# Sums of squares of a layer norm: from VectorE reductions to TensorE products in column groups, in the output stage of a fused triangle and spectral kernel

## The chip, the cores and the metric

One core of a Trainium2 chip runs the whole kernel. The metric is the device time of one execution in microseconds. A core has five engines with a queue each: TensorE (PE, with its weight loads as PEld), VectorE (DVE), ScalarE (ACT), GpSimd (POOL) and SyncE (SP, which here issues DMAs). An engine runs its queue in order, and waits at an instruction until what it needs has been signalled.

## The reference

The input x is 512 x 512 tokens of 64 channels, in f32. Two layers follow one another, each added to its input after a group norm (`_gn`) over the whole image:

```python
# layer 0, on xn = layer norm of the group-normed x
left  = (xn @ left_w  + left_b)  * mask * sigmoid(xn @ lgate_w + lgate_b)
right = (xn @ right_w + right_b) * mask * sigmoid(xn @ rgate_w + rgate_b)
out_gate = sigmoid(xn @ ogate_w + ogate_b)
out = einsum('bkjd,bkid->bijd', left, right)
out = _ln(out, onorm_w, onorm_b) @ out_w + out_b
x = x + out * out_gate
# layer 1: 12 x 12 lowest Fourier modes of the group-normed x, mixed over channels, and back
x = x + real(ifft2(mix(fft2(_gn(x))[:12, :12])))
```

The mask is 1 where both tokens of a pair are valid; the sum over k runs over valid rows alone, and a masked output pair is the layer norm of zero, so that its `out` is one constant row.

## The kernel before, in words

Rows with a valid mask, at most 256 of 512, are ranked to the front, so that the triangle product is computed in a 256 x 256 square ("compact"). The kernel runs in stages: statistics of x and copying of the valid tokens; the projections left and right; the triangle product; the stage of u; the output stage; the spectral mixing; and the last stage, which adds the inverse transform and writes the output. The change lies in the stage of u (686 to 794 us in the profile) and, above all, in the output stage (794 to 1485 us).

**Steps and units.** The code that does both stages is one loop over steps, `for s in range(-LEAD, total_g + 2 * SIZE)`. A step handles 8 tokens of each of 128 rows, 512 columns of a tile; eight steps (`SIZE`) make a unit of 64 tokens by 128 rows. The first 8 units (`first`) belong to the stage of u: they apply the output norm and out_w to the triangle product and write the result to u in memory (`u_d`). The 32 others are the output stage. A unit is a pair (jc, half): 32 columns jc of the image, and two of the four blocks of 128 ranked rows. Blocks 0 and 1 hold the valid rows, blocks 2 and 3 the masked ones. Before, half 0 was blocks 0 and 1 and half 1 was blocks 2 and 3, and half 1 came first, save for the last jc. A unit is also split into four chunks c of 16 tokens: c 0 and 1 are its first block, c 2 and 3 its second.

**What a step does**, with the line of the profile:

- TensorE transposes four 128x128 squares of the input of step s+13 into PSUM (`t_ps`, L969), and ScalarE copies them out, minus the mean of the group norm, as `xt_c` (L974).
- TensorE multiplies `xt_c` of step s by the gate's weights: `w_ps`, four matmuls in which `xt_c` is the stationary operand and `gate_x` moves (L979, in `times`).
- TensorE centers the channels of step s+12 in the same manner with the matrix `center_x`: `c_ps` (L979, in `centered`). The tokens are then on the partitions and the channels along the free axis. ScalarE squares it (L1004), and in every second step VectorE sums the squares over the channels of two steps (L1012, into `scratch`).
- Once a unit, at step 5, ScalarE takes the root of the sums (L1018), and VectorE the reciprocal at step 7 (L1188): the factor `rs_n` of the layer norm. ScalarE must load another table for the root and again for the sigmoid that follows.
- VectorE multiplies `w_ps` by the factor (L1195) and in odd steps adds the gate's bias (L1201) to get `z_t` of a chunk. ScalarE takes its sigmoid in even steps (L1146).
- GpSimd multiplies `z_t` by u, or by the row `bias_row_out` in masked blocks (L1038, `gated`), and adds the result to the input that lies in `places` (L1042, `added`). It also issues the gathers of the next input (L629).
- TensorE takes the Fourier transform over the rows of the unit before: `f_ps`, at steps 0 and 4, as four matmuls of 512 columns in the four groups of 32 columns of the array (L1069, `tile_position`); ScalarE copies it out every second unit (L1077).
- VectorE gathers statistics for the second group norm (L1097), four instructions a step, and joins them once in four units.
- SP loads the slots of u for jc+1 (L1029, 32 DMAs of 64 KB) at step 4 of every second unit, and stores finished tiles (L1058).

**What sets the order.** The block runs under `tc.manual_schedule()`: each engine gets its instructions in the order in which the loop writes them. Within a step ScalarE's order is xt_c, the sigmoid (even steps), the root (step 5), the square, the copy of f_ps. TensorE's is t_ps, w_ps, c_ps, f_ps.

**Buffers.** PSUM[...]: t_ps 2, scratch 1, f_ps 1, c_ps 2, w_ps 2. `z_t` has four buffers in SBUF, sq_c two of 16 x 64.

## Time and profile before

| What | us |
|---|---|
| median of 3 runs (1837.78 to 1840.75) | 1838.84 |
| profiled execution, whole time | 1839.54 |
| its span on the core | 1837.7 |
| stage of u in it | 686 to 794 |
| output stage in it | 794 to 1485 |
| TensorE busy in the span | 1637.7 (89%) |
| VectorE busy | 1423.6 (77%) |
| ScalarE busy | 961.9 (52%) |
| GpSimd busy | 945.3 (51%) |

The span runs from the first to the last instruction of the program, and 1.8 us of the profiled time lie around it. Busy shares are of the whole span; what binds one stage must be read inside it. A row of the profile's groups gives line, engine, operation, what is written and read, shapes and count, then the busy time and the mean of one instruction in ns. A row of a timeline has the start in us, the length in us, and the group; `x8` are eight instructions run together. An f32 matmul leaves two records[...], so four matmuls read as x8; a transpose leaves one.

### The profile page before, as it was taken

The numbers are of one execution on the slowest core, as the hardware profiler recorded it, in microseconds if no ns is written. First come the engines' busy times: TensorE is split into PE (matmuls) and PEld (weight loads), VectorE is DVE, ScalarE is ACT, GpSimd is POOL, SyncE is SP. The second block draws the span as 40 slices with busy tenths as digits, with TensorE's granted clock in tenths as the row PEclk, the third lists the DMA queues.
The fourth block names the chain that finished last, engine by engine and source line by source line (L and its number), as shares of the span: only waits on it lengthen the run. The fifth ranks groups of instructions, "written<-read, shape, count | busy, mean of one in ns | idle before, by whom it ended". The sixth has DMA issues, their size and how long they took to land.

```text
span 1837.7 us, 33577 instructions
## 1 busy us (share of the span) xinstructions
PE 1637.7 (89%) x11414; PEld 1287.7 (70%) x11414; DVE 1423.6 (77%) x2973; ACT 961.9 (52%) x1708; POOL 945.3 (51%) x711
## 2 busy tenths in 40 slices
PE   6779799999799999999999999999999866998772
PEld 5667666665678878897788888888888744665441
DVE  5989777777455547788999999999999975675552
ACT  3555555555222259976777777777777631111000
POOL 3666211111000006788999999999999862211110
PEclk9989899999899999999999999999999966555555
DMA  6999255556656513667777876776777698999999
GB/s 255 381 375 371 106 127 138 138 138 154 208 174 182 177 41 141 224 234 257 254 244 249 279 269 233 241 274 234 253 258 258 210 273 338 411 426 426 427 427 379
DMA packets 188453, 467.94 MB, mean 255 GB/s; under 512 B 34672, under 2 KB 134000, under 8 KB 147184
## 3 DMA queue, kind: packets, MB, share of 16 engines
q1 hardware_dynamic: 157376, 262.21, 42.5%
q0 software_dynamic: 27712, 201.40, 29.1%
q10 hardware_dynamic: 3184, 2.08, 0.4%
q8 instruction: 93, 1.52, 0.3%
q14 instruction: 88, 0.72, 0.1%
HBM read 278.05 MB, written 187.56 MB: 253 GB/s over the span
## 4 chain that ended last, share of the span: by engine, by line
PE 29%; DVE 16%; DMA 9%; POOL 4%; issue 3%; ACT 1%; DVEq 0%; POOLq 0%; ACTq 0%
PE c_ps L979 6%; PE w_ps L979 6%; PE t_ps L969 5%; PE l_ps L1348 4%; DVE stats2c L1097 4%; DMA places<-x_h,dst_i 4%; PE y_ps L990 4%; DVE z_t L1195 3%; DVE scratch L1012 3%; DVE z_t L1201 3%; PE f_ps L1069 2%; POOL z_t L1038 2%; DMA out_x<-places 2%; POOL places L1042 2%; DMA lx_t<-x_h,dst_i 2%
## 5 line engine op out<-in xcount | busy, mean ns | idle before, releaser
L979 PE MATMUL w_ps<-gate_x,xt_c 128*128 128x128 f32 x2048 | 280.1, 280 | 32.1 <-DVE z_t L1195 26.7
L1042 POOL TENSOR_TENSOR places<-places,z_t 128x1024 f32<-128x1024 f32 x127 | 301.2, 2371 | 8.0
L979 PEld LDWEIGHTS w_ps<-gate_x,xt_c 128*128 128x128 f32 x2048 | 251.5, 194 | 47.8 <-DVE z_t L1195 43.4
L979 PE MATMUL c_ps<-center_x,xt_c 128*128 128x128 f32 x2048 | 276.2, 278 | 1.2 <-ACT xt_c L1008 0.6
L979 PEld LDWEIGHTS c_ps<-center_x,xt_c 128*128 128x128 f32 x2048 | 252.1, 194 | 3.9 <-ACT xt_c L974 2.3
L1348 PE MATMUL l_ps<-places,rinv 24*128 24x512 f32 x512 | 207.8, 1124 | 29.3 <-DVE places L1355 18.6
L1097 DVE BATCH_NORM_STATS2 stats2c<-places 128x6 f32<-128x128 f32 x1024 | 220.5, 278 | 12.5 <-POOL places L1042 12.5
L1012 DVE TENSOR_REDUCE scratch<-sq_c 128x16 f32<-128x1024 f32 x160 | 194.6, 1216 | 27.9 <-ACT sq_c L1007 18.7
L1146 ACT ACTIVATE z_t<-z_t 128x1024 f32<-128x1024 f32 x128 | 135.5, 1059 | 133.7 <-DVE z_t L1201 116.0
L1199 POOL TENSOR_TENSOR z_t<-z_t,bias_row_out 128x1024 f32<-128x1024 f32 x32 | 75.7, 2365 | 246.6 <-DVE z_t L1195 242.5
L969 PE MATMUL t_ps<-c_ident,places 128*128 128x128 f32 x1280 | 199.0, 278 | 1.3 <-DVE places L854 1.3
L1348 PEld LDWEIGHTS l_ps<-places,rinv 24*128 24x128 f32 x512 | 120.3, 303 | 111.9 <-DVE places L1355 59.6
L969 PEld LDWEIGHTS t_ps<-c_ident,places 128*128 128x128 f32 x1280 | 144.5, 142 | 60.6 <-issue 50.3
L974 ACT ACTIVATE xt_c<-t_ps,ab_xc 128x512 f32<-128x512 f32 x256 | 176.0, 687 | 10.7 <-PE t_ps L969 9.8
L1195 DVE TENSOR_TENSOR z_t<-w_ps,rs_n 128x512 f32<-128x512 f32 x256 | 171.9, 672 | 3.7 <-PE w_ps L979 3.5
L1004 ACT ACTIVATE sq_c<-c_ps 128x512 f32<-128x512 f32 x256 | 150.5, 588 | 30.9 <-PE c_ps L979 29.4
L679 DVE BATCH_NORM_STATS2 stats1c<-x_ps 128x6 f32<-128x512 f32 x256 | 155.6, 681 | 12.5 <-PE x_ps L678 12.2
L1201 DVE TENSOR_TENSOR z_t<-z_t,scratch 128x1024 f32<-128x1024 f32 x128 | 156.3, 1221 | 10.0 <-ACT rs_n L1018 3.8
L1038 POOL TENSOR_TENSOR z_t<-z_t,places 128x1024 f32<-128x1024 f32 x64 | 151.6, 2369 | 16.2 <-ACT z_t L1146 13.3
L1355 DVE TENSOR_TENSOR places<-places,l_ps 128x512 f32<-128x512 f32 x176 | 110.2, 683 | 56.1 <-DMA places<-x_h,dst_i 45.5
L1038 POOL TENSOR_TENSOR z_t<-z_t,bias_row_out 128x1024 f32<-128x1024 f32 x63 | 149.4, 2371 | 4.6 <-ACT z_t L1146 4.0
L733 POOL COPY rbc<-rq_out 128x512 f32<-128x512 f32 x64 | 38.3, 613 | 210.0 <-DVE rq_out L209 132.0
(212 smaller groups left out, 2748.8 us busy)
## 6 DMA issues: line engine op xcount, KB each, us to landing
x_h<-places SPq DMA_DIRECT2D x64, 1024.0 KB
out_x<-places SPq DMA_DIRECT2D x44, 1024.0 KB
places<-u_d SPq DMA_DIRECT2D x512, 64.0 KB
out_x<-lx_t SPq DMA_DIRECT2D x20, 1024.0 KB
left_d<-o_c SPq DMA_DIRECT2D x64, 256.0 KB
right_d<-o_c SPq DMA_DIRECT2D x64, 256.0 KB
left_raw<-left_d SPq DMA_DIRECT2D x64, 256.0 KB
right_raw<-right_d SPq DMA_DIRECT2D x64, 256.0 KB
```

Of the source, the lines that this page charges most:

```text
L679: nc.vector.bn_stats(stats[:, 0, 16 * (jc % quarter) + 4 * r + c, :], ps.rearrange("p i k -> p (i k)"))
L969: nc.tensor.transpose(tps[:, i, :], flat[:, o : o + P], ident)
L974: nc.scalar.activation(xts[s], tps, AF.Identity, bias=ab1[:, 2:3])
L979: nc.tensor.matmul(ps[:, 2 * i : 2 * i + 2, :], xts[s][:, i, :], w, start=True, stop=True)
L1004: nc.scalar.activation(sq, cps, AF.Square)
L1012: nc.vector.tensor_reduce(totals[k % 2][:, 8 * (n - 1) : 8 * (n + 1)], sqs.pop(s // 2), AX.X, ALU.add)
L1038: nc.gpsimd.tensor_mul(zs[k, c], zs[k, c], u)
L1042: nc.gpsimd.tensor_add(xr, xr, zs.pop((k, c)))
L1097: nc.vector.bn_stats(st[k // 4][:, g, k % 4, :], x_of(k)[:, :, 2 * g : 2 * g + 2])
L1195: nc.vector.tensor_mul(z[:, 8 * odd : 8 * odd + 8, :], wps, rs)
L1201: nc.vector.tensor_add(z, z, bias_ps["ogate"].unsqueeze(1).to_broadcast([P, 16, C]))
L1348: nc.tensor.matmul(ps.rearrange("p j o -> p (j o)"), rinv[h, b, :], it[h], start=True, stop=True, tile_position=(32 * g, 0),)
```

## The change

Centering in the output stage is turned around: `center_x` is the stationary operand and `xt_c` moves, so that one matmul of 512 columns makes `c_ps` with the channels on the partitions. ScalarE squares it as before. In the next step TensorE sums the squares over channels with four matmuls, one for each of the four squares of 128 tokens, in the four groups of 32 columns: the stationary operand `sum_w[:, n, :]` (128 x 32) puts the sums of step n in rows 2n and 2n+1 of its group, and the eight steps of a unit are accumulated in one bank, `row_sums`. At step 4 ScalarE copies that bank to SBUF, at step 5 TensorE turns it with one transpose into a buffer of `t_ps`, and ScalarE takes the root from there. The bank comes from c_ps, which has one buffer now. ScalarE's square stands ahead of the root in step 5.

A unit now holds one block of valid rows and one of masked rows (`block`), in the order half 0, half 1, save for the last jc, which is as before. VectorE makes the product of chunk 3 (masked, `shared`), 30 times in all, and GpSimd the other three. In the stage of u the reductions stay on VectorE but run on one step each.

```diff
-            units = [(jc, half) for jc in range(NJ) for half in ((1, 0) if jc < NJ - 1 else (0, 1))]
+            units = [(jc, half) for jc in range(NJ) for half in (0, 1)]
...
+                sum_w = lp.tile([P, SIZE, 32], F32, name="sum_w")
+                nc.scalar.dma_start(sum_w, t["c_sum_w"])
+
+                def block(k, r):
+                    jc, half = units[k]
+                    return half + 2 * r if jc < NJ - 1 else 2 * half + r
...
                     def centered(s):
                         if s >= first * SIZE:
-                            return times(ps_c, "c_ps", s, center_x)
+                            ps = ps_c.tile([P, 4, P], F32, name="c_ps")
+                            nc.tensor.matmul(ps, center_x, xts[s], start=True, stop=True)
+                            return ps
...
                     def summed(s):
                         k, n = divmod(s, SIZE)
-                        nc.vector.tensor_reduce(
-                            totals[k % 2][:, 8 * (n - 1) : 8 * (n + 1)], sqs.pop(s // 2), AX.X, ALU.add
-                        )
+                        nc.vector.tensor_reduce(totals[k % 2][:, 8 * n : 8 * n + 8], sqs.pop(s), AX.X, ALU.add)
+
+                    def summed_rows(s):
+
+                        k, n = divmod(s, SIZE)
+                        if n == 0:
+                            row_sums[k] = ps_r.tile([P, P], F32, name="row_sums")
+                        sq = sqs.pop(s).rearrange("p n c -> p (n c)")
+                        for i in range(4):
+                            nc.tensor.matmul(
+                                row_sums[k][32 * i : 32 * i + 32, :], sum_w[:, n, :], sq[:, i * P : (i + 1) * P],
+                                start=(n == 0), stop=(n == SIZE - 1), tile_position=(0, 32 * i),
+                            )
+
+                    def keep_rows(k):
+                        kept[k] = small.tile([P, P], F32, name="kept_rows", bufs=1)
+                        nc.scalar.copy(kept[k], row_sums.pop(k))
+
+                    def turn_rows(k):
+                        tps = ps_t.tile([P, 4, P], F32, name="t_ps")[:, 0, :]
+                        nc.tensor.transpose(tps, kept.pop(k), ident)
+                        by_token[k] = tps.rearrange("p (i n) -> p i n", i=4)[:, :, : 2 * SIZE]
...
+                    def shared(k, c):
+
+                        return c == 3 and block(k, 1) >= 2 and k < last
...
-                            ps_c = products.enter_context(tc.tile_pool(name="np_c", bufs=2, space=PSUM))
+                            ps_c = products.enter_context(tc.tile_pool(name="np_c", bufs=1, space=PSUM))
+                            ps_r = products.enter_context(tc.tile_pool(name="np_r", bufs=1, space=PSUM))
                             ps_w = products.enter_context(tc.tile_pool(name="np_w", bufs=2, space=PSUM))
                         if 0 <= s < total_g:
                             wps = raw(s) if k < first else times(ps_w, "w_ps", s, gate_x)
                             del xts[s]
+                        if n == 5 and first <= k + 1 < first + len(units):
+                            turn_rows(k + 1)
                         if 0 <= s + LEAD - 1 < total_g:
                             cps = centered(s + LEAD - 1)
+                        if first * SIZE <= s + LEAD - 2 < total_g:
+                            summed_rows(s + LEAD - 2)
                         if n in (0, 4) and held(1):
                             transform(v - 1, n // 4)
...
+                        if cps is not None:
+                            squared(s + LEAD - 1, cps)
+                        if n == 4 and first <= k + 1 < first + len(units):
+                            keep_rows(k + 1)
                         if n == 5 and 0 <= k + 1 < first + len(units):
                             root(k + 1)
-                        if cps is not None:
-                            squared(s + LEAD - 1, cps)
...
-                            if held(i) and (v - i, c) != (last, 3):
+                            if held(i) and (v - i, c) == (last, 3):
+                                finished()
+                            elif held(i) and not shared(v - i, c):
                                 gated(v - i, c)
                             elif held(i):
-                                finished()
+                                nc.vector.tensor_mul(
+                                    zs[v - i, c], zs[v - i, c], bias_ps["out"].unsqueeze(1).to_broadcast([P, 16, C])
+                                )
...
-                        if 0 <= s + LEAD - 2 < total_g and (s + LEAD - 2) % 2 == 1:
+                        if 0 <= s + LEAD - 2 < first * SIZE:
                             summed(s + LEAD - 2)
```

Loads, stores, the gate and the transform take their row block from `block(k, r)` instead of `2 * half + r`. `sq_c` has three buffers of 8 x 64.

## The prediction

> **What bounds the kernel now.** I read the slices of the page first, to find the stage that the change touches, then the busy time of the engines in that stage, its waits, and two timelines in it. The slices (40 of 46 us each) put the output stage in slices 17 to 32:
>
> ```profile
> PE   6779799999799999999999999999999866998772
> DVE  5989777777455547788999999999999975675552
> POOL 3666211111000006788999999999999862211110
> PEclk9989899999899999999999999999999966555555
> ```
>
> PE, DVE and POOL all show nines there and the clock is full, so taking work from one engine pays only as far as the next allows. The busy times of the steady part (26 units of 8 steps) say how near the three are; the columns are length, then PE, PEld, DVE, ACT and POOL busy:
>
> ```profile
> 883.00:1452.50 569.50, 550.66 (x4649) 486.97 (x4649) 558.61 (x1314) 422.56 (x626) 541.15 (x261) 0.99 0.74 254
> ```
>
> A unit lasts 569.5/26 = 21.9 us, in which DVE is busy 21.5, POOL 20.8, ACT 16.3. PE's 550.7 holds pipelined tails, so I take PE from starts instead (below): 20.1. The waits of the same stretch agree that DVE is the one all others wait for:
>
> ```profile
> ACT z_t L1146 <- DVE z_t L1201: 92.4, 65, 2.6
> PE w_ps L979 <- DVE z_t L1195: 13.5, 16, 2.0
> ```
>
> So **VectorE bounds it, by little**: PE has some 1.8 us of slack in a unit. The change takes from DVE and gives to PE, so the PE prices decide. PE's timeline (start, length, group), one step with f_ps and one without:
>
> ```profile
> 1178.92 1.06 PE L979 MATMUL c_ps<-center_x,xt_c 128*128 128x128 f32 x8
> 1179.90 1.07 PE L1069 MATMUL f_ps<-places,hb 128*32 128x512 f32 x8
> 1180.90 0.66 PE L969 MATMUL t_ps<-c_ident,places 128*128 128x128 f32 x4
> 1181.39 1.06 PE L979 MATMUL w_ps<-gate_x,xt_c 128*128 128x128 f32 x8
> 1182.29 1.06 PE L979 MATMUL c_ps<-center_x,xt_c 128*128 128x128 f32 x8
> 1183.18 0.60 PE L969 MATMUL t_ps<-c_ident,places 128*128 128x128 f32 x4
> ```
>
> From start to start: t_ps 0.437 us (median over the stage), w_ps 0.893, c_ps 0.893. A plain step is 2.22. f_ps is the only product here in four column groups: c_ps lasts 0.987 ahead of it (0.094 more), f_ps itself 0.996, and the t_ps after it 0.494 (0.057 more). Its two passes start 0.453 apart. A pass of 256 columns (tri_c_ps) takes 0.2155, so 512 columns stream in about 0.427; two passes are 0.853, and entering and leaving the column groups adds 0.094 + 0.026 + 0.116 + 0.057 = 0.29 us. A unit has two f_ps: 8 x 2.22 + 2 x 1.15 = 20.1 us.
>
> **What the Trainium skill says.** "TensorEngine Tiling (Array Packing)", Key Properties: changing the tiling mode drains TensorE, while different tiles run in parallel. The trace agrees: four groups of 512 columns take one group's streaming time, plus the 0.29 us just found. "ScalarE: Activation LUTs", What ACT_TABLE_LOAD costs: 1283 ns and a drain of about 1380 for each switch of set. The trace has the 1283, but the next ACTIVATE starts 12 ns later, so I use 1.28 alone.
>
> **The change, part by part**, for one unit.
>
> c_ps with fixed weights: 8 x (4 matmuls of 128 columns) become 8 x 1 of 512. By tri_c_ps a pass of 512 is 2 x 0.2155 = 0.431, so c_ps is 0.862 instead of 0.893; the weight loads it drops were hidden beside matmuls already. Gain 8 x 0.031 = 0.25 us.
>
> Row sums on PE: in every step four matmuls of 128 columns in four column groups, between c_ps and t_ps, both of the full array. Streaming 2 x 0.107 plus the 0.29 of entering and leaving is 0.51 us; x 8 = 4.1 us. Bounds: 0.39 if the 0.094 and 0.026 of entering belong to f_ps's own waits; 1.15 if groups this short do not overlap (4 x 0.213 + 0.29). Nothing points below 0.21, the streaming itself. I take 0.51. In steps 0 and 4, f_ps now follows the sums in the same mode and pays 0.88 instead of 1.15 in all: with its two, 1.76.
>
> The turn of the sums is one transpose, 0.11. Its wait on ScalarE's copy is covered: the copy is issued a step earlier, some 2 us before.
>
> PE's unit is then 8 x (0.437 + 0.893 + 0.862 + 0.507) + 1.76 + 0.11 = **23.5 us**, against 21.9 of the whole stage now.
>
> DVE: four reductions go (104 in the stretch, 126.0 us busy, 4.85 a unit), one product of 1.22 comes: 21.5 - 4.85 + 1.22 = 17.9. POOL loses one product of 2.37: 18.4. ACT gains the copy of 128x128, about 0.3 by the 128x64 root of 0.31: 16.6. None binds, so what these three win is worth nothing once PE takes 23.5.
>
> **The added wait.** c_ps goes from two buffers to one, so each c_ps waits for the square of the step before. ScalarE around the root, now:
>
> ```profile
> 1204.56 1.28 ACT L1018 ACT_TABLE_LOAD   x1
> 1205.85 0.31 ACT L1018 ACTIVATE rs_n<-scratch,eps 128x64 f32<-128x64 f32 x1
> 1206.07 0.59 ACT L1004 ACTIVATE sq_c<-c_ps 128x512 f32<-128x512 f32 x1
> 1206.54 0.59 ACT L1077 COPY places<-f_ps 128x512 f32<-128x512 f32 x1
> 1207.01 0.71 ACT L974 ACTIVATE xt_c<-t_ps,ab_xc 128x512 f32<-128x512 f32 x1
> 1207.74 1.28 ACT L1146 ACT_TABLE_LOAD   x1
> 1209.03 1.06 ACT L1146 ACTIVATE z_t<-z_t 128x1024 f32<-128x1024 f32 x1
> 1209.99 0.58 ACT L1004 ACTIVATE sq_c<-c_ps 128x512 f32<-128x512 f32 x1
> ```
>
> After the change the square of step 5 comes first, then load, root, (f_ps copy in every second unit), xt_c, load, sigmoid, square of step 6. Let c_ps of step 5 end streaming at 0. Its square starts at 0.2 (0.16 of the array's tail and 0.04 of signal) and frees ACT at 0.7; load 1.98, root 2.2, xt_c 2.78, load 4.08, sigmoid 5.05, square done at 5.65; with the f_ps copy 6.1. PE: sums, t_ps and w_ps of step 6 end at 1.84, c_ps at 2.70, and it is at c_ps of step 7 after another 1.84, at 4.54. It stalls 1.1 us, or 1.6 with the copy: **1.4 us a unit**. Behind c_ps in PE's order stand the sums, t_ps and the next w_ps, so DVE waits too and nothing is made up. Bounds: 0 if xt_c, sigmoid and square need not follow so closely, 2 if signals cost more. The other steps are clear: their even ones have the square done 1.0 us before it is needed.
>
> Unit after: 23.5 + 1.4 = **24.8 us**.
>
> **The order of blocks.** Every unit now has one gated block that reads u and one that takes the bias row. u of the first jc is needed in unit 0 step 3, not unit 1. SP's issues (64 in 43 us, some of the second set) and POOL's wait for the first set:
>
> ```profile
> 804.83 43.43 SPq L1029 DMA_DIRECT2D places<-u_d  x64
> 830.96 2.36 POOL L1038 TENSOR_TENSOR z_t<-z_t,places 128x1024 f32<-128x1024 f32 x1 [2.71 <-DMA places<-u_d]
> ```
>
> They start at 804.8, after the last u is written, whatever the order of units. POOL now has unit 0 done at 822.4. In the new order its first product waits for 16 of 32 slots (the sixteenth is issued at 813, landing about 821), its second for all, until 831. z has four buffers, so unit 1 is held: its step 2 gets a buffer at 831 + 2 x 2.37 = 835.7. PE, two steps ahead through w_ps's two buffers, is at step 4 there and at unit 2 after 4 x 3.1 us, at 848.5, instead of 833. **16 us, once**; bounds 5 (POOL's slack makes some up) and 22. Later sets are issued at step 4 of an even unit and needed at step 3 of the next even one, 15 steps or 45 us on; 32 issues take 19 us and land in 7, so they stay hidden. Gathers and stores keep their number and size.
>
> **Costed at nothing.** In the u stage (686 to 794 us) 32 reductions become 64 shorter ones: DVE is busy 86.8 of 108 us there, PE 106.5, so PE covers it; without that cover the fixed part of a reduction, under 0.1 us x 32, is 3 us. sum_w is one load on ACT's queue, hundreds of us ahead of its use. POOL's lighter load shortens the end by 2 us at most, as the last two units keep all their POOL work.
>
> **Sum.** PE is fully loaded from unit 2 to step 3 of unit 30, 28.4 units: 28.4 x 24.8 = 704 us, against 1459 - 833.5 = 625.5 now: +79. With +16 and -2: +93. On the profiled execution's 1839.5 (span 1837.7 and 1.8 around it, 0.7 above the median of the runs) that is **1933 us**.
>
> **Rivals.** (A) Entering and leaving column groups is hidden, as the weights of the sums are constant, and no stall shows. Then PE's unit is 8 x 2.405 + 1.87 = 21.1 and with 0.2 of waits 21.3: 28.4 x (21.3 - 22.0) = -20, and with half the head, +8: about 1828, faster. For it: DVE and POOL really do fall to 18. Against it: all f_ps of the stage pay the 0.29. It decides where sums and stall together stay below 2.1 us a unit: the break-even unit is 22.0 - 14/28.4 = 21.5, and 19.4 of it is all the rest. That is 0.26 a step, less than the switches alone. (B) The sums cost 0.51 but ScalarE's chain does not hold c_ps: 28.4 x 23.5 = 667, +42 + 14: about 1895. For it: the order puts the root behind the square. (C) Groups of 128 columns run one after another: 0.64 x 8 x 28.4 = 145 more, about 2078. Against it: f_ps starts its four groups within 20 ns. That the reductions stay on DVE is not possible: the program no longer has them in this stage.
>
> **Numbers.** Chances: my sum 0.50, B 0.29, C 0.06, A 0.12, no change 0.03 (A with the full 16 of the head). So faster 0.12, same 0.03, slower 0.85, with 0.2%, about 3.7 us, as what a measurement of this kernel can tell from no change. The range takes in B with its lower bounds (sums 0.41, half the stall) and my sum with signals costing more: 1850 to 1980; it leaves out A and C.
>
> **What would show it.** Right: PE without idle but at c_ps, waiting for ACT sq_c, once a unit; t_ps starting 0.5 us after the first row_sums; DVE and POOL waiting for PE; units of 24 to 25 us; POOL's wait for u near 815 to 831. Wrong: units near 21 us with DVE or POOL still full, row_sums of 0.25 us, or c_ps never waiting for ACT.

## The result, and the profile after

| | before | after |
|---|---|---|
| median, runs on the same chip | 1838.31 us (1833.35 to 1840.75) | 1957.87 us (1956.31 to 1960.05) |
| ratio, 95% interval | | 1.0662 [1.0641, 1.0683] |
| span of the profiled execution | 1837.7 | 1954.4 |
| unit 2 starts (VectorE's reciprocal of its factor) | 833.5 | 852.9 |
| from there to unit 31 | 638.9 | 736.2 |
| the rest | 365.3 | 365.3 |

The change costs 6.6%. The last three rows split the 116.7 us between the two spans: 19.4 are lost ahead of unit 2, 97.3 over the next 29 units (25.4 us a unit instead of 22.0), and nothing after them. A run can be split like this wherever one instruction marks each turn of a loop; here it is the reciprocal, one for each unit.

The slices of the page after, a slice being 48.9 us. In slices 17 to 33 the nines of DVE and POOL have become sevens, while PE keeps its own:

```profile
PE   6779899998999999899999999999999975898873
DVE  6889677775555478367777777767777784676542
POOL 3665111110000057577777677777777773111110
PEclk9989899998999999999999999999999996555555
```

The busy times of 26 steady units (columns as in the prediction: length, PE, PEld, DVE, ACT, POOL) give 18.8 us a unit for DVE, 18.5 for POOL and 17.2 for ACT, of a unit of 25.5. VectorE and GpSimd were relieved and now idle for more than a quarter of each unit, so the loss sits in the engine that took the work or in one that it waits for:

```profile
877.90:1541.00 663.10, 627.43 (x5093) 390.02 (x5092) 488.17 (x1231) 448.21 (x650) 480.89 (x234) 0.99 0.63 214
```

The waits of the stage from 900 to 1550 us say who (total, times, longest). VectorE now waits for TensorE, where it was the other way round, and TensorE's matmuls wait above all for the square of the single `c_ps`, 23 times:

```profile
DVE z_t L1243 <- PE w_ps L986: 147.0, 115, 3.5
...
PE c_ps L992 <- ACT sq_c L1010: 35.7, 23, 1.8
```

TensorE's timeline shows both prices. L1029 are the sums of a step:

```profile
1204.02 1.02 PE L992 MATMUL c_ps<-xt_c,center_x 128*128 128x512 f32 x2
1204.97 0.43 PE L1029 MATMUL row_sums<-sq_c,sum_w 128*32 128x128 f32 x8
1205.33 0.66 PE L976 MATMUL t_ps<-c_ident,places 128*128 128x128 f32 x4
1205.82 1.06 PE L986 MATMUL w_ps<-gate_x,xt_c 128*128 128x128 f32 x8
1206.71 1.02 PE L992 MATMUL c_ps<-xt_c,center_x 128*128 128x512 f32 x2
...
1208.52 1.06 PE L986 MATMUL w_ps<-gate_x,xt_c 128*128 128x128 f32 x8
1210.85 1.12 PE L992 MATMUL c_ps<-xt_c,center_x 128*128 128x512 f32 x2 [1.27 <-ACT sq_c L1010]
```

From start to start a plain step is 2.70 us (1204.02 to 1206.71), and the eight records of the sums, 0.214 us of streaming, take 0.505 of it: 0.094 more on `c_ps`, 0.356 of their own, 0.056 more on `t_ps`. In step 7 of the unit `w_ps` to `c_ps` is 2.33 instead of 0.893. ScalarE's timeline says why: the square of step 6 (1210.21) stands behind the root, two table loads and the sigmoid, and `c_ps` starts 0.06 us after it ends:

```profile
1205.14 0.60 ACT L1010 ACTIVATE sq_c<-c_ps 128x512 f32<-128x512 f32 x1 [1.23 <-PE c_ps L992]
1205.75 1.28 ACT L1048 ACT_TABLE_LOAD   x1
1207.05 0.32 ACT L1048 ACTIVATE rs_n<-t_ps,eps 128x64 f32<-128x64 f32 x1
1207.26 0.68 ACT L981 ACTIVATE xt_c<-t_ps,ab_xc 128x512 f32<-128x512 f32 x1
1207.96 1.28 ACT L1188 ACT_TABLE_LOAD   x1
1209.25 1.06 ACT L1188 ACTIVATE z_t<-z_t 128x1024 f32<-128x1024 f32 x1
1210.21 0.58 ACT L1010 ACTIVATE sq_c<-c_ps 128x512 f32<-128x512 f32 x1
```

### The profile page after: what moved, and what is told of

The parts are those of the page before. It is cut to its first block, busy times and chain, and to the rows that moved or that the text cites. A ratio compares the mean times of both kernels' runs of the same rounds, so it can differ in the third digit from the quotient of the medians.

```text
span 1954.4 us, 34397 instructions
## 1 busy us (share of the span) xinstructions
PE 1730.5 (89%) x11958; PEld 1164.1 (60%) x11958; DVE 1343.2 (69%) x2907; ACT 994.2 (51%) x1740; POOL 877.2 (45%) x681
## 3 DMA queue, kind: packets, MB, share of 16 engines
q8 instruction: 97, 1.59, 0.3%
## 4 chain that ended last, share of the span: by engine, by line
PE 48%; DMA 13%; POOL 11%; issue 8%; ACT 7%; DVE 6%; SPq 5%; POOLq 0%; ACTq 0%; DVEq 0%
PE tri_c_ps L850 7%; POOL places L1080 5%; DMA places<-x_h,dst_i 4%; PE c_ps L992 4%; PE t_ps L976 4%; PE w_ps L986 3%; PE y_ps L999 3%; PE l_ps L1396 3%; PE sides_c L747 3%; POOL z_t L1072 3%; PE x_ps L678 3%; PE cc_ps L716 3%; PE gates_c L747 3%; SPq L1063 3%; SPq L637 2%
## 5 line engine op out<-in xcount | busy, mean ns | idle before, releaser
L1243 DVE TENSOR_TENSOR z_t<-w_ps,rs_n 128x512 f32<-128x512 f32 x256 | 176.4, 689 | 201.2 <-PE w_ps L986 193.3
L992 PE MATMUL c_ps<-xt_c,center_x 128*128 128x512 f32 x512 | 267.0, 603 | 42.1 <-ACT sq_c L1010 41.3
L986 PE MATMUL w_ps<-gate_x,xt_c 128*128 128x128 f32 x2048 | 275.7, 278 | 6.3 <-DVE z_t L1243 6.3
L976 PE MATMUL t_ps<-c_ident,places 128*128 128x128 f32 x1280 | 211.3, 288 | 1.3 <-DVE places L854 1.3
L976 PEld LDWEIGHTS t_ps<-c_ident,places 128*128 128x128 f32 x1280 | 135.5, 141 | 98.3 <-issue 87.4
L1247 POOL TENSOR_TENSOR z_t<-z_t,bias_row_out 128x1024 f32<-128x1024 f32 x32 | 75.5, 2364 | 248.0 <-DVE z_t L1243 245.1
L1029 PEld LDWEIGHTS row_sums<-sq_c,sum_w 128*32 128x32 f32 x2048 | 40.3, 108 | 194.6 <-issue 171.0
L664 ACT COPY xc<-xg 128x128 f32 x352 | 105.0, 298 | 66.5 <-POOL xc L664 43.9
L850 PE MATMUL tri_c_ps<-left_t,right_t 128*128 128x256 f32 x512 | 128.5, 395 | 5.4 <-ACT right_t L844 0.8
```

The source lines that it names most:

```text
L850: nc.tensor.matmul(ps[:, r, :], rt[:, kb, r * P : (r + 1) * P], lt[:, kb, :], start=(kb == 0), stop=(kb == 1))
L976: nc.tensor.transpose(tps[:, i, :], flat[:, o : o + P], ident)
L986: nc.tensor.matmul(ps[:, 2 * i : 2 * i + 2, :], xts[s][:, i, :], w, start=True, stop=True)
L992: nc.tensor.matmul(ps, center_x, xts[s], start=True, stop=True)
L1243: nc.vector.tensor_mul(z[:, 8 * odd : 8 * odd + 8, :], wps, rs)
```

## The experiments

Theory: TensorE bounds, at 23.4 us of its own work, the switches of column groups being the larger part of what was added; the single `c_ps` adds a stall; the order of blocks costs once. Rivals: the waits alone, or the new sums alone, or the order alone carry the loss. Ratios are to the kernel before, run beside each.

### The stall: ScalarE's square of step 6 ahead of the sigmoid (e9_square_first)

```diff
+                        if cps is not None and n == 6:
+                            squared(s + LEAD - 1, cps)
                         if n % 2 == 0:
...
                                 nc.scalar.activation(zs[v - i, c], zs[v - i, c], AF.Sigmoid)
-                        if cps is not None:
+                        if cps is not None and n != 6:
```

> The changed kernel, with ScalarE's square of step 6 put ahead of the sigmoid and its table load in that step; nothing else. Theory (one c_ps buffer makes TensorE wait for ScalarE's chain once a unit): TensorE idle before c_ps, released by sq_c, is 41 us in the changed kernel; the square now comes 2.3 us sooner, so this idle falls below 5 us and the time falls by about 40 to 47 us, to 1911 to 1918. Rival (TensorE's instructions alone set 25 us a unit and the wait only shows where the slack is, or the wait moves to the sums or to the sigmoid's readers): less than 15 us, 1943 or more.

1908.10 us, ratio 1.0406 [1.0387, 1.0425]. Against the 1.0662 of the change that is 2.6%, 47 us: more than a third of the loss hung on the place of one ScalarE instruction. In step 7 `c_ps` now follows `w_ps` by 0.90 us, where it was 2.33:

```profile
1208.64 1.06 PE L986 MATMUL w_ps<-gate_x,xt_c 128*128 128x128 f32 x8
1209.54 1.02 PE L992 MATMUL c_ps<-xt_c,center_x 128*128 128x512 f32 x2
```

Units are 23.4 us, and 23.8 where the copy of `f_ps` falls in, so the 23.4 that TensorE's starts add up to is now the unit itself.

### The stall from the other side: two buffers for c_ps (e1_two_c)

```diff
-                ) as s1, tc.tile_pool(name="np_n", bufs=1, space=PSUM) as ps_n, ...
+                ) as s1, ...
-                    scratch = ps_n.tile([P, 4, P], F32, name="scratch")
+                    scratch = s1.tile([P, 4, P], F32, name="scratch")
-                            ps_c = ...(tc.tile_pool(name="np_c", bufs=1, space=PSUM))
+                            ps_c = ...(tc.tile_pool(name="np_c", bufs=2, space=PSUM))
```

To free a bank, `scratch`, which also holds the bias row that VectorE adds, moves to SBUF (and the input has one buffer less).

> The changed kernel with two c_ps buffers again; the bank comes from scratch, which moves to SBUF. Theory (the wait is ScalarE's chain, and c_ps is only its first reader on TensorE): c_ps of step 7 no longer waits, but the row sums of step 7 need the same square of step 6 one c_ps later, so 0.86 us of the 1.5 to 1.7 us of stall go, some 24 us in 28 units: about 1933, with TensorE waiting for ScalarE at the sums instead. Rival (the single buffer alone is the cause): the whole 41 to 47 us go, 1911 to 1918. Rival (neither): 1958, and slower if VectorE reads the bias from SBUF more slowly.

1980.50 us, ratio 1.0812 [1.0794, 1.0830], slower than the change. The buffer did its part: `w_ps` to `c_ps` is 0.893 at the median, with no wait for a square left. The wait went on to the sums: the matmuls of `row_sums` now wait for `sq_c`, 25.4 us in 38 times from 900 to 1540 us, and their weight loads 61.9 us in 46. But the move of `scratch` spoiled the test: the bias addition doubled. The group is first shown in the change, then here, from 900 to 1460 us (busy, mean ns, idle before):

```profile
L1249 DVE TENSOR_TENSOR z_t<-z_t,scratch 128x1024 f32<-128x1024 f32 x88 | 107.4, 1221 | 9.3 <-ACT set_mean L1146 6.6
```

```profile
L1249 DVE TENSOR_TENSOR z_t<-z_t,scratch 128x1024 f32<-128x1024 f32 x89 | 221.8, 2492 | 3.0
```

### That confounder alone, on the kernel before (e12_before_sbuf)

```diff
-                    scratch = ps_n.tile([P, 4, P], F32, name="scratch")
+                    scratch = s1.tile([P, 4, P], F32, name="scratch")
```

The pool of that bank goes, and one buffer of the input, as in e1_two_c.

> The kernel before with scratch (factors, sums and the two bias rows) in SBUF instead of PSUM; nothing else is moved. It measures what the run with two c_ps buffers met: the bias addition of VectorE took 2481 ns there instead of 1221, and additions of GpSimd 2766 instead of 2368. Theory (VectorE with both operands in SBUF waits for GpSimd): the bias addition takes about 2.4 us here too, 1.2 us x 4 a unit more on the engine that bounds it, 120 us or more above the kernel before. Rival (it came from the changed form alone, such as squares held longer): within 10 us of it.

1956.57 us, ratio 1.0658 [1.0626, 1.0691]: as much as the whole change costs. Groups from 900 to 1460 us, of before and then with `scratch` in SBUF:

```profile
L1042 POOL TENSOR_TENSOR places<-places,z_t 128x1024 f32<-128x1024 f32 x103 | 244.4, 2373 | 6.6
...
L1201 DVE TENSOR_TENSOR z_t<-z_t,scratch 128x1024 f32<-128x1024 f32 x103 | 125.8, 1221 | 8.0 <-ACT rs_n L1018 2.9
```

```profile
L1042 POOL TENSOR_TENSOR places<-places,z_t 128x1024 f32<-128x1024 f32 x88 | 261.2, 2968 | 5.6
...
L1201 DVE TENSOR_TENSOR z_t<-z_t,scratch 128x1024 f32<-128x1024 f32 x87 | 193.7, 2227 | 3.0
```

Only the place of `scratch` changed (and the input's spare buffer went), and both VectorE's addition and GpSimd's got longer. The Trainium skill, "GPSIMD Engine Reference", Key points, says that the two share SBUF interfaces and collide when a VectorE instruction has two SBUF inputs; the runs agree, with 1.22 us becoming 2.23 and GpSimd's 2.37 becoming 2.97. The trace of this run also says that it is the two at once, and not SBUF or the missing buffer: 2 of the 128 additions of VectorE run beside no arithmetic of GpSimd and take 1.22 us, as before, while the other 126 take at least 1.59; and GpSimd's additions take 2.37 us where none of these runs beside them (24), and 3.11 where one does (103). So e1_two_c says nothing on what two buffers are worth.

### The switches: sums of four steps at once, beside f_ps (e4_fours)

```diff
-                        if first * SIZE <= s + LEAD - 2 < total_g:
-                            summed_rows(s + LEAD - 2)
+                        if first * SIZE <= s + LEAD - 2 < total_g and (s + LEAD - 2) % 4 == 3:
+                            for q in range(4):
+                                summed_rows(s + LEAD - 2 - 3 + q)
```

`sq_c` has five buffers for it.

> The changed kernel with the row sums of four steps made together, at steps 0 and 4, where f_ps is in column groups anyway. The same matmuls are made. Theory (entering and leaving the column groups costs 0.29 us each time, whatever is done there): six of eight changes of mode go, 1.76 us a unit, but TensorE then reaches c_ps of step 7 about 1.0 us sooner and waits that much longer for ScalarE; net 0.75 us a unit, about 21 us, 1937, with t_ps to w_ps back at 0.44 us in six steps of eight and the idle before c_ps up to about 70 us. Rival (the price lies in the matmuls and their weight loads, not in the change of mode): 1958, and the sums at steps 0 and 4 take four times the present 0.51 us.

1939.28 us, ratio 1.0579 [1.0562, 1.0597], 15 us less than the change. One entry into the column groups, shared with `f_ps`, now serves four steps, and the sums of four steps take 0.897 us: streaming, and little else.

```profile
1213.13 1.06 PE L986 MATMUL w_ps<-gate_x,xt_c 128*128 128x128 f32 x8
1214.02 1.02 PE L992 MATMUL c_ps<-xt_c,center_x 128*128 128x512 f32 x2
1214.98 1.08 PE L1029 MATMUL row_sums<-sq_c,sum_w 128*32 128x128 f32 x32
1215.88 1.04 PE L1106 MATMUL f_ps<-places,hb 128*32 128x512 f32 x8
1216.85 0.65 PE L976 MATMUL t_ps<-c_ident,places 128*128 128x128 f32 x4
...
1220.53 1.02 PE L992 MATMUL c_ps<-xt_c,center_x 128*128 128x512 f32 x2
1221.75 0.66 PE L976 MATMUL t_ps<-c_ident,places 128*128 128x128 f32 x4 [0.19 <-ACT rs_n L1048]
1222.24 1.06 PE L986 MATMUL w_ps<-gate_x,xt_c 128*128 128x128 f32 x8
1225.66 0.70 PE L992 MATMUL c_ps<-xt_c,center_x 128*128 128x512 f32 x1 [2.36 <-ACT sq_c L1010]
```

Six of eight entries are saved, 6 x 0.29 = 1.7 us a unit, but only 0.7 arrives (units 24.2 and 24.7 instead of 24.9 and 25.4): TensorE reaches step 7 sooner, ScalarE is no sooner done, and the mean wait of `c_ps` for its square grows from 1.55 us (35.7 in 23) to 2.15 (49.5 in 23). Another 0.36 goes where `t_ps` of step 7 waits for the root, which reads the turned sums out of one of its two buffers (`c_ps` to `t_ps` 1.22 us, from 1220.53, instead of 0.861). More than half of what the switches gave, ScalarE's queue took.

The 0.7 holds for undisturbed units, and the time of the run shows less of it. In this trace twelve of the 29 units from unit 2 on have a granted clock of 0.92 to 0.96, where the others have 1.00, and are about 1.7 us longer (26.4 for 24.7, 25.9 for 24.2). The change's trace has three such spells. Why there are more here is open.

### The order: blocks as before (e5_order), and mixed blocks on the kernel before (e6_mixed)

```diff
-            units = [(jc, half) for jc in range(NJ) for half in (0, 1)]
+            units = [(jc, half) for jc in range(NJ) for half in ((1, 0) if jc < NJ - 1 else (0, 1))]
...
-                    return half + 2 * r if jc < NJ - 1 else 2 * half + r
+                    return 2 * half + r
```

> The changed kernel with the units of before again: half 1 (blocks 2 and 3) ahead of half 0 (blocks 0 and 1); VectorE keeps chunk 3 of the masked units, 15 products instead of 30. Theory (the first u arrives late for the new order, once): GpSimd's wait of 18.7 us for u goes, unit 2 starts about 17 us sooner, and units of 25 us follow as in the changed kernel: about 1941. Rival (the late start is made up afterwards): 1955 to 1958. Rival (the 15 products that go back to GpSimd make it the bound): units above 25.3 us, 1950 or more.

1942.34 us, ratio 1.0602 [1.0581, 1.0623], 11 us less than the change. From the first unit of the u stage, unit 2 starts after 154.0 us instead of 164.5 (146.8 before). So the order costs 10.5 us, and 7.2 of the head remain without it: units 0 and 1 are slower themselves. GpSimd's timeline of the change has the wait for u:

```profile
817.13 2.36 POOL L1072 TENSOR_TENSOR z_t<-z_t,places 128x1024 f32<-128x1024 f32 x1 [18.73 <-DMA places<-u_d]
...
826.95 2.34 POOL L1072 TENSOR_TENSOR z_t<-z_t,places 128x1024 f32<-128x1024 f32 x1 [3.94 <-DMA places<-u_d]
```

The mixed order and VectorE's product alone, with centering and sums as before (`units`, `block` and `shared` of the diff, nothing else of it):

```diff
-            units = [(jc, half) for jc in range(NJ) for half in ((1, 0) if jc < NJ - 1 else (0, 1))]
+            units = [(jc, half) for jc in range(NJ) for half in (0, 1)]
...
+                            elif held(i) and not shared(v - i, c):
+                                gated(v - i, c)
                             elif held(i):
-                                finished()
+                                nc.vector.tensor_mul(zs[v - i, c], zs[v - i, c], ...)
```

> The kernel before with one part of the change alone: units of one valid and one masked block, and VectorE makes chunk 3's product of 30 units; reductions, centering and buffers stay as before. Theory (VectorE bounds the kernel before, at 21.5 of 21.9 us a unit, and the first u comes late for the new order): VectorE gets 1.22 us a unit more, so units take 22.9 to 23.1 us, some 30 us in all, and the head adds about 14: 40 to 48 us above the kernel before. Rival (GpSimd at 20.8 us was the bound, and gains 2.37 us a unit): faster than before but for the head, at most 14 us above it.

1882.61 us, ratio 1.0263 [1.0235, 1.0291]. Unit 2 starts at 850.2 instead of 833.5, and the units take 22.8 us instead of 22.0: where VectorE is the bound, each product that it takes from GpSimd counts. So that part of the change could pay only if the other part first made VectorE idle, without a new bound in its place.

### All three remedies on the change (e10_four_sq_order)

The edits of e9_square_first, e4_fours and e5_order together, with the copy of `f_ps` moved to step 6.

> The changed kernel with its three extra costs taken back together: sums of four steps at steps 0 and 4, the square ahead of the sigmoid in step 6 (and f_ps copied out at step 6, not 5), the order of units of before. Theory (the loss is changes of mode, ScalarE's chain and the first u, and adds up): TensorE's unit is 8 x (0.437 + 0.893 + 0.861) + 2 x 2.02 + 0.11 = 21.7 us, plus 0.3 to 0.5 of waits, against 21.9 before: 5 to 20 us above the kernel before. Rival (further costs of the new form stay, in weight loads, PSUM or VectorE): 35 us or more above it.

1893.56 us, ratio 1.0313 [1.0287, 1.0338]: 58 us above the kernel before, as the rival had it, and units of 23.1 and 23.6, not 22. The costs that the rival named are not seen, though. Without its waits TensorE's own work is the 21.7 us a unit that were expected (eight steps of 2.19, 2.02 more for each of the two places with sums and `f_ps`, and the turn, 0.11). Its waits for ScalarE come on top, 1.0 us a unit for the square, from 900 to 1540 us, and 0.35 for the root:

```profile
PE c_ps L992 <- ACT sq_c L1010: 23.7, 23, 1.2
```

Even without them 21.7 would stand against the 21.9 of the whole unit before, a gain of 0.2 us a unit at best. So moving all sums to TensorE has next to nothing to gain in this stage: it makes TensorE what VectorE was.

### Half of the sums

If two engines are nearly full, halves should pay. Four of the eight steps keep before's centering and VectorE's reduction; the order is that of before, and the square of step 6 goes first.

First version: TensorE takes steps 4 to 7 of a unit, VectorE steps 0 to 3 (e11_half).

```diff
+                        if s >= first * SIZE and s % SIZE < 4:
+                            return times(ps_c, "c_ps", s, center_x)
...
+                        if first * SIZE <= s + LEAD - 2 < total_g and (s + LEAD - 2) % SIZE == 7:
+                            for q in range(4):
+                                summed_rows(s + LEAD - 2 - 3 + q)
...
-                        if 0 <= s + LEAD - 2 < first * SIZE:
+                        if 0 <= s + LEAD - 2 < total_g and (s + LEAD - 2 < first * SIZE or (s + LEAD - 2) % SIZE < 4):
                             summed(s + LEAD - 2)
```

> A mixture of both kernels, on top of the three repairs: in each unit the first four steps are centered by tokens and reduced by VectorE as before, the other four by channels and summed by TensorE, all at step 4 beside f_ps; two roots of 128x32 instead of one. Theory (three engines lie within 2 us of one another, so work is to be split, not moved): TensorE 17.5 + 0.1 + 2.02 + 1.15 + 0.11 = 20.9 us a unit, VectorE 21.5 - 2.4 + 0.6 = 19.7, GpSimd 19.6; with 0.4 of waits 21.3 against 21.9, so 10 to 20 us below the kernel before. Rival (the coupling of engines in order costs what the split saves): within 5 us of it.

1940.08 us, ratio 1.0569 [1.0543, 1.0594], a miss with a new wait of almost 5 us in a unit: VectorE's first reduction of the next unit, into `scratch`, stands behind ScalarE's root, which reads another part of `scratch`:

```profile
1217.95 0.69 DVE L1022 TENSOR_REDUCE scratch<-sq_c 128x8 f32<-128x512 f32 x1 [4.90 <-ACT rs_n L1050]
```

The Trainium skill, "PSUM — Partial Sum Buffer", PSUM bank collisions raise a hardware error, asks for semaphores that guard PSUM by bank (and block of 32 partitions), not by address. The wait fits that, but a guard on the whole tile would look the same; no run here tells the two apart.

Second version: the halves change places, and VectorE reduces into SBUF (e13_half2).

```diff
-                        if s >= first * SIZE and s % SIZE < 4:
+                        if s >= first * SIZE and s % SIZE >= 4:
                             return times(ps_c, "c_ps", s, center_x)
...
+                            by_dve[k] = small.tile([P, 32], F32, name="part", bufs=2)
+                        to = totals[k % 2][:, 8 * n : 8 * n + 8] if k < first else by_dve[k][:, 8 * n - 32 : 8 * n - 24]
+                        nc.vector.tensor_reduce(to, sqs.pop(s), AX.X, ALU.add)
```

The turned sums are copied to SBUF too, so that they hold no buffer of `t_ps` until the root.

> A second mixture. The first one lost to waits that its trace names: VectorE's reductions of step 5 write the bank of scratch, which ScalarE's root is reading (107 us), and t_ps and c_ps wait for ScalarE. Here the first four steps of a unit are centered by channels and summed by TensorE together at step 0, turned at step 1 and copied to SBUF by ScalarE there; the last four are centered by tokens and reduced by VectorE into SBUF; two roots of 128x32 at step 5 read SBUF alone. The order of units is that of before, the square precedes the sigmoid in step 6, f_ps is copied out at step 6. Theory (with the waits gone, the split counts): TensorE 20.9 us a unit, VectorE 19.7, GpSimd 19.6, some 0.5 us of waits: 21.4 against 21.9, 8 to 18 us below the kernel before. Rival (the waits of a single c_ps buffer for ScalarE stay and eat it): 0 to 30 us above the kernel before, with TensorE idle ahead of c_ps or w_ps.

1878.13 us, ratio 1.0230 [1.0204, 1.0256]: 42 us above the kernel before, over the rival's range too. The wait for the root is gone; the wait of the single `c_ps` for its square, which the rival named, is left, from 900 to 1540 us, 1.25 us a unit of 23.0:

```profile
PE c_ps L986 <- ACT sq_c L1012: 28.8, 23, 1.5
```

Third version: the row sums live in a buffer of `t_ps`, which frees a bank for a second `c_ps`; the sums stand behind `f_ps`, and its copy at step 4 (e14_half_two_c).

```diff
-                            row_sums[k] = ps_r.tile([P, P], F32, name="row_sums")
+                            row_sums[k] = ps_t.tile([P, 4, P], F32, name="t_ps")
...
-                            ps_c = products.enter_context(tc.tile_pool(name="np_c", bufs=1, space=PSUM))
-                            ps_r = products.enter_context(tc.tile_pool(name="np_r", bufs=1, space=PSUM))
+                            ps_c = products.enter_context(tc.tile_pool(name="np_c", bufs=2, space=PSUM))
```

> The second mixture with two c_ps buffers, which the trace of the last run asks for: TensorE was idle ahead of c_ps, released by sq_c, for 42 us in 26 units, at steps 0 and 1, since ScalarE runs late there after its two table loads. The four sums of a unit are now made at one step, so they and their turned form live for two steps in a buffer of t_ps, and c_ps has both banks again. The sums follow f_ps in step 0, and f_ps is copied out at step 4. Theory: the 1.6 us a unit of waits go, TensorE comes to 20.9 us a unit plus 0.3, and VectorE, GpSimd and ScalarE stay below 20: 21.2 us against 21.9, 10 to 22 us below the kernel before. Rival (ScalarE's lateness moves to the sums, which need the square of step 7, or to t_ps): half of it stays, units of 22 us, within 8 us of the kernel before.

1838.69 us, ratio 1.0034 [1.0022, 1.0047]: 6 us above the kernel before, which is the rival's range. Units take 22.3 us, where it has 22.0. Against the second version that is 2% of the time, for the second buffer of `c_ps` together with the new order of sums and copy; no run tells them apart. Busy times from 900 to 1460 us, 25.1 units: 21.6 us a unit for PE with its tails, 20.1 for DVE, 19.6 for POOL:

```profile
900.00:1460.00 560.00, 542.88 (x4727) 433.63 (x4728) 505.22 (x1284) 431.11 (x682) 492.38 (x239) 1.00 0.72 248
```

One wait of TensorE's matmuls was left that comes every unit, of `c_ps` for the copy `xt_c` that stands behind the second table load and the sigmoid:

```profile
PE c_ps L986 <- ACT xt_c L981: 16.4, 23, 0.8
```

Two more runs tried to take it away. The sigmoid of step 6 behind the copy and square of step 7, and VectorE's product at the end of step 1 (e15_half_late):

```diff
-                        if n % 2 == 0:
+                        if n in (0, 2, 4):
                             i, c = (0, n // 2 - 1) if n >= 2 else (1, 3)
...
+                        if n == 7 and held(0):
+                            nc.scalar.activation(zs[v, 2], zs[v, 2], AF.Sigmoid)
...
-                                nc.vector.tensor_mul(zs[v - i, c], zs[v - i, c], ...)
+                                todo = zs[v - i, c]
```

> As e14_half_two_c, with two edits of order alone: the sigmoid that stood in step 6 of a unit is issued in step 7, behind that step's copy xt_c and square, so that xt_c of the last step no longer stands behind the second table load; and VectorE's shared product is issued at the end of step 1. In e14_half_two_c the wait 'c_ps L986 <- ACT xt_c L981' took 20.8 us of 23 units, 0.83 to 1.0 us a unit. Theory: that wait was all that stood between the split and a gain; it goes, the units fall from 22.3 to about 21.4 us, and 28 of them give 23 to 25 us: about 1810 to 1818 us, a ratio of 0.988 to 0.992 to the kernel before. Rival: the sigmoid was late already, and moved behind it the gate, GpSimd's products and the rows to be kept are late next; then the units stay at 22 us or more, a ratio of 1.000 to 1.006, and another wait of about 1 us a unit is in the list of waits.

1853.98 us, ratio 1.0115 [1.0090, 1.0140]. The wait is nearly gone (3.8 us are left of the 16.4), and the rival was right in kind, with a larger loss than it gave: GpSimd waits 51.3 us for the late sigmoid, and VectorE's statistics wait 41.0 us for GpSimd:

```profile
POOL z_t L1082 <- ACT z_t L1206: 51.3, 25, 5.5
...
DVE stats2c L1144 <- POOL places L1090: 41.0, 18, 3.2
```

Centering, sums and root one step later (e16_half_lag):

```diff
-                        if 0 <= s + LEAD - 1 < total_g:
-                            cps = centered(s + LEAD - 1)
+                        if 0 <= s + LEAD - 2 < total_g:
+                            cps = centered(s + LEAD - 2)
...
-                        if n == 5 and 0 <= k + 1 < first + len(units):
+                        if n == 6 and 0 <= k + 1 < first + len(units):
                             root(k + 1)
```

> As e14_half_two_c, but centering, squares, sums, the copy and turn of the sums and the root all run one step later (c_ps is made of the xt_c of the step before the last, no longer of the one just copied), so that the root stands behind the sigmoid of step 6 and the two table loads of a unit lie two steps apart. In e14_half_two_c the wait 'c_ps L986 <- ACT xt_c L981' took 0.7 to 0.9 us of every unit of 22.3. Theory: ScalarE's lateness at its two table loads is what is left, and a step of slack covers it without moving the sigmoid (which e15_half_late showed to cost more than it gave). The sums no longer adjoin f_ps and cost 0.15 more; so the units fall by 0.5 to 0.7 us, 14 to 20 us in all: 1813 to 1824 us, a ratio of 0.990 to 0.995 to the kernel before. Rival: the units stand at TensorE's own work (some 21.2 us) and at VectorE and GpSimd within 1.5 us of it, so that any order has one of them late: the reciprocal, which now has a step less after the root, holds VectorE instead, and the time stays within 6 us of e14_half_two_c, a ratio of 1.000 to 1.006.

1867.96 us, ratio 1.0179 [1.0151, 1.0208]. Both missed: the reciprocal does wait for the root, 22 times, as the rival had it, but the time is far above the rival's too.

```profile
DVE rs_n L1250 <- ACT rs_n L1062: 30.3, 22, 2.4
```

With all of TensorE, VectorE and GpSimd between 19.6 and 21.6 us of a unit of 22.3, in both runs the delay that was taken from one of them was met by another. No version here beats the kernel before; whether another order of ScalarE's queue would is open.

## Why the prediction was right, step by step

- **What binds.** That VectorE bounded by little, and that TensorE would take its place, is shown by the reversed waits. GpSimd is busy 18.5 us a unit (18.4 predicted), ScalarE 17.2 (16.6), VectorE 18.8 (17.9). The instructions of VectorE overlap: the busy times of its groups add up to 46 us more than its own in the stretch of before, and to 24 us more in that of after, where it idles between them. So taking 126 us of reductions away freed less than 126.
- **c_ps with fixed weights.** (A "pass" in the prediction is one of the two records that an f32 matmul leaves.) A step of 0.437 + 0.893 + 0.862 + 0.507 = 2.699 was predicted, and 2.697 measured. The small gain is there.
- **The row sums.** 0.505 us measured, 0.51 predicted; with `f_ps` behind them `f_ps` adds 0.858 where 0.88 was predicted. Rival A (switches hidden) and C (groups one after another) are out. e4_fours shows it by the other way: four steps for one entry take 0.897 us in place of 4 x 0.505.
- **TensorE's unit.** 23.5 predicted. From the starts of the change it is 8 x 2.697 + 2 x 0.858 + 0.109 = 23.4, and e9_square_first runs at it.
- **The added wait.** The mechanism is as described; rival B (no stall) is out, and its number is e9_square_first, 1908 us where 1895 was given. The size was too small: 1.44 and 1.93 us instead of 1.1 and 1.6. In the timeline above, the square ahead of the first table load lasts 0.61 us until the load starts, and the copy ahead of the second 0.70; the prediction let them take 0.5 and 0.58, as if what follows them began before they end, which a table load didn't do. That is 0.23 us; the square also starts 0.06 us later. Over 29 units the 0.3 is 9 us.
- **The head.** 16 us predicted for the order, and 17.7 found (19.4, less the 1.7 by which this execution's u stage came later). That the total is right is luck. u came some 4 us sooner than predicted, at 817.13 and 826.95, and what held TensorE was not a buffer of `z_t`: `f_ps` of unit 0 waited for the rows that GpSimd adds.

```profile
831.76 1.92 PE L1106 MATMUL f_ps<-places,hb 128*32 128x512 f32 x4 [6.79 <-POOL places L1080]
```

The sum's last step also slips a little: 835.7 + 4 x 3.1 is 848.1, not 848.5. And the parts differ: on the kernel before the order costs 16.6 (e6_mixed, 163.4 us instead of 146.8 from the first unit of the u stage), on the changed one 10.5 (e5_order), because units 0 and 1 are slower themselves and take 7.2 already. The sum counted TensorE's new rate only from unit 2.
- **Costed at nothing.** The fixed part of a reduction is 0.16 us, not under 0.1 (one step takes 0.695 us, two 1.228). But TensorE covers it, as was said: from the first to the last reciprocal the stage of u takes 93.0 us, and 94.8 before.
- **Left out: the column basis.** The sum held TensorE's steps but not the products of the column basis (L902), which come three times in the stage and take 2.7 us each. In the change they cost less than that, since ScalarE catches up meanwhile and the next `c_ps` does not wait:

```profile
1310.05 0.42 PE L1029 MATMUL row_sums<-sq_c,sum_w 128*32 128x128 f32 x8
1310.41 2.86 PE L902 MATMUL t_ps<-col_basis,places 128*128 128x24 f32 x24
1313.11 0.64 PE L976 MATMUL t_ps<-c_ident,places 128*128 128x128 f32 x4
1313.58 1.06 PE L986 MATMUL w_ps<-gate_x,xt_c 128*128 128x128 f32 x8
1314.47 1.02 PE L992 MATMUL c_ps<-xt_c,center_x 128*128 128x512 f32 x2
```

The undisturbed pair of units with such products takes 29.2 + 22.3 instead of 25.4 + 24.9, 1.2 us more; three make 4 us. In e9_square_first, which has no such wait to save, the same pair takes 27.6 + 22.3 instead of 23.8 + 23.4, the full 2.7.
- **Left out: a slower clock.** The prediction read the clock as full. Three times in these 29 units TensorE runs at about half its pace for some 3 us, and the granted clock of the unit falls to 0.94 to 0.98; here `w_ps` takes 1.70 us to the next start instead of 0.893:

```profile
1288.94 1.92 PE L986 MATMUL w_ps<-gate_x,xt_c 128*128 128x128 f32 x8
1290.64 1.47 PE L992 MATMUL c_ps<-xt_c,center_x 128*128 128x512 f32 x2
```

Each spell costs 1.6 or 1.7 us, 5 us in all. The kernel before has units with a clock of 0.93 too, but there VectorE is the bound, and they take 23.9 us beside 23.7 for the same kind of unit at 1.00. What brings the spells is open.
- **The end.** 2 us of gain were taken, none came: the time from unit 31 to the end is 365.3 in both.

Of the 24 us between +93 and the 116.7 of the spans these make 23: 9 for the stall, 5 for the clock, 4 for the column basis, 3 in the head and 2 at the end. The last one is not assigned.

## What to carry to other kernels

Where VectorE is busy 21.5 us of a unit of 21.9 and GpSimd 20.8, relieving VectorE alone can gain little: before moving work, add up what the receiver must do in a turn, switches of mode and rare operations included, and stop where it comes near the old turn. When a buffer is taken away, look at the queue of the engine that frees it, not at its busy share: ScalarE was busy two thirds of the time and still held TensorE 1.7 us a unit, and putting one instruction ahead of another won two fifths of the loss back. And an experiment that moves an operand between PSUM and SBUF tests that move as well.

## What the runs showed of the hardware that was not expected

An ACTIVATE that follows another starts about 0.1 us before the record of the first ends (1207.26 beside 1207.05 + 0.32), but no table load between 700 and 1500 us did, in any run: each begins at least 17 ns after the end of the instruction ahead of it. Entering and leaving the column groups cost 0.29 us with 0.853 us of streaming in them (`f_ps`) and with 0.214 (the sums of a step) alike. VectorE's addition of 128x1024 f32 went from 1.22 to 2.23 us on average when its second operand came from SBUF beside a busy GpSimd; with that placement, and one input buffer less, 121 us of 1835 were lost. And a short spell of slower clock cost a unit 1.7 us where TensorE was the bound, and 0.2 where VectorE was.
